# Layer 1's last step with its loads made during the convolution before it, and its additions on two engines

## The chip, the cores and the metric

The kernel runs on one core of a Trainium2 chip, in one launch. The metric is the device time in microseconds (us) of that core. Five engines work side by side, each through its own queue of instructions in order: PE multiplies matrices, DVE (vector), ACT (scalar) and POOL (GpSimd) do elementwise work, SP only issues DMA transfers. ACT and POOL can issue DMAs as well.

## The reference, cut to what matters

The input x has 4 batches of 128 channels and 64 x 64 = 4096 positions. Four layers follow each other.

- Layer 0: a projection, a causal convolution of width 4, a selective scan over the 4096 positions with 16 states for each of 256 inner channels, a gate, an output projection, and the residual. Its result is x1.
- Layer 1: x1 is normalized in groups of channels, an incidence matrix between positions (distance under 16) is built for each batch, and a hypergraph convolution gives `out`. Then comes a batch norm over all batches and positions, and Silu:

```python
mean = jnp.mean(out, axis=(0, 2, 3))
var = jnp.var(out, axis=(0, 2, 3))
y = gamma * (out - mean) * rsqrt(var + eps) + beta
return y * sigmoid(y)          # and x = x1 + this
```

- Layer 2: tokens (positions x channels); linear attention with a layer norm ahead of it, then a mixture of experts.
- Layer 3: windowed attention without softmax, then a mixture of experts.

The mean and variance of layer 1 are over all four batches, so no element of layer 1's result can be made before the convolution of the last batch is done.

## The kernel before

The kernel is written in a framework that records instructions with the tiles they read and write. It takes tiles from pools, places the pools in SBUF (the on-chip memory of 128 partitions), sets the semaphores, and orders each engine's queue when the kernel is built. A tile of a pool takes the room of an earlier one when that one's readers are done. In the built program each DMA also carries one of eight completion counters and is issued only when the DMA before it on that counter has landed, so at most eight are under way.

**Layers 0 and 1** (`layers01`) are interleaved: `layer0` is a generator that makes the scan in steps, `layer1(b)` one that makes the convolution of batch b, and the loop at the end runs layer 0 of batch b + 1 beside layer 1 of batch b. For the last batch (b = 3) layer 0 is done and `layer1(3)` runs alone. Its pools are `aw` (weights and the tiles xn0 to xn7 of the normalized batch), `l0p` (layer 0's tiles, in two to six buffers), `l0bc` (rows of B and C for the scan), `l1t` (layer 1's tiles), and PSUM and DRAM pools. All of them stay open until `layers01` ends.

`layer1(b)` begins with a few small operations for the group norm (`ps_gm`, `ps_gv`, `rstd`), then loads x1 of its batch in eight chunks of 512 columns from DRAM (`xn`, L457, SP's queue) and normalizes each on ACT (L458). A chunk's tile is free when the previous batch has read it last, in `mean` (L631, POOL). The square of chunk 7 (`sq`, L463) is what the first matmul of the convolution waits for, `ps_hb` in `row` (L490). The comparisons, turns, edges and `ps_v` (L622) follow. `finish` stores each chunk of the result to the DRAM tensor hg (L635, SP's queue) and collects statistics.

At the end of `layers01` the batch norm's scale and bias are made from the statistics (`bn`, L666 to L671).

**Layer 1's last step** (`layer1_end`) works in 16 units, one for each batch and 1024 columns. A unit loads o (1024 columns of hg) on ACT's queue (L683) and x (the same columns of x1) on SP's queue (L685), 512 KB each; ACT makes Silu of o with scale and bias (L686); POOL adds o to x (L687); PE turns x in eight transpositions of 128 columns into two PSUM tiles `ps_x` (L692); ACT copies the first PSUM tile and DVE the second into X (L694), the token tile of 64 KB for each partition that layers 2 and 3 work on. Both o and x have three buffers.

Then the first two groups of expert weights of layer 2 are loaded (`load`: `w1` and `w2f`, 1 MB each, on SP's queue, and `b1` on ACT's), and `attn2` starts: its statistics over X (`lnst`, L702), its weight W (L740), normalized tiles z (L779, L781), and projections `ps_qk` (L789).

Of the kernel before, what the change touches and what calls it, by code (L numbers as in the profile page):

```python
# [7 lines left out]
F32 = mybir.dt.float32  # L8
F16 = mybir.dt.float16
FP8 = mybir.dt.float8e4  # L10
AF = mybir.ActivationFunctionType
ALU = mybir.AluOpType
AX = mybir.AxisListType
PSUM = bass.MemoryType.PSUM
DRAM = bass.MemoryType.DRAM

P = 128
B = 4
# [22 lines left out]
class Net:  # L41
# [33 lines left out]
    def layers01(self):  # L75
        nc, tc, a = self.nc, self.tc, self.a
# [9 lines left out]
        LAG = 6 * 2  # L86
        with ExitStack() as ctx:
            wp = ctx.enter_context(tc.tile_pool(name="aw", bufs=1))
            w2 = ctx.enter_context(tc.tile_pool(name="l0p", bufs=2))
            bcp = ctx.enter_context(tc.tile_pool(name="l0bc", bufs=5))  # L90
            tp = ctx.enter_context(tc.tile_pool(name="l1t", bufs=2))
            dp = ctx.enter_context(tc.tile_pool(name="l0d", bufs=3, space=DRAM))
            ip = ctx.enter_context(tc.tile_pool(name="l1i", bufs=1, space=DRAM))
# [2 lines left out]
            ps = ctx.enter_context(tc.tile_pool(name="aps", bufs=4, space=PSUM))  # L96
# [103 lines left out]
            def due(every=False):  # L200
                for w in list(waiting):
                    if every or w[0] <= self.tick:
                        waiting.remove(w)
                        w[1]()
# [445 lines left out]
            for b in range(B):  # L650
                l1 = layer1(b)
                if b < B - 1:
                    done = 0
                    for k in range(states):
                        next(l0, None)
                        self.tick += 1
                        due()
                        while done * states < work * (k + 1):
                            done += next(l1)
                for _ in l1:  # L660
                    self.tick += 1
                    due()
# [7 lines left out]
            nc.vector.tensor_tensor(bn[:, 1:2], bn[:, 2:3], bn[:, 0:1], ALU.mult)  # L670
            nc.vector.tensor_tensor(bn[:, 1:2], gb[:, 1:2], bn[:, 1:2], ALU.subtract)  # L671

    def layer1_end(self):

        nc = self.nc
        with self.tc.tile_pool(name="l1e", bufs=3) as tp, self.tc.tile_pool(
            name="l1eps", bufs=4, space=PSUM
        ) as ps:
            for b in range(B):
                for c in range(4):  # L680
                    sl = slice(c * 1024, (c + 1) * 1024)
                    o = tp.tile([P, 1024], F32, tag="o", name="o")
                    nc.scalar.dma_start(o, self.hg[b][:, sl])  # L683
                    x = tp.tile([P, 1024], F32, tag="x", name="x")
                    nc.sync.dma_start(x, self.x1[b][:, sl])  # L685
                    nc.scalar.activation(o, o, AF.Silu, scale=self.bn[:, 0:1], bias=self.bn[:, 1:2])  # L686
                    nc.gpsimd.tensor_tensor(x, x, o, ALU.add)  # L687
                    for h in range(2):
                        pt = ps.tile([P, 4, P], F32, tag="tr", name="ps_x")
                        for i in range(4):  # L690
                            k = 4 * h + i
                            nc.tensor.transpose(pt[:, i, :], x[:, k * P : (k + 1) * P], self.ident)  # L692
                        k = 8 * c + 4 * h
                        (nc.vector.tensor_copy if h else nc.scalar.copy)(self.X[:, b, k : k + 4, :], pt)  # L694


    def ln_stats(self, sp, b, j0, n, rs=None):
# [543 lines left out]
@with_exitstack  # L1241
def tile_kernel(ctx: ExitStack, tc: tile.TileContext, a, out):
    net = Net(tc, a)
    net.setup(ctx)
    net.layers01()
    xp = ctx.enter_context(tc.tile_pool(name="X", bufs=1))
    net.X = xp.tile([P, B, NB, P], F32, tag="X", name="X")
    net.ew = ctx.enter_context(tc.tile_pool(name="fe", bufs=2))
    net.layer1_end()
    net.ahead = [net.load("L2_ffn", g) for g in range(2)]  # L1250
    net.attn2()
    net.ffn("L2_ffn")
    net.ahead = [net.load("L3_ffn", g) for g in range(2)]
    net.attn3()
    net.ffn("L3_ffn", out)
# [48 lines left out]
```

## Time and profile before

| what | value |
|---|---|
| median of 3 runs | 4328.91 us (4327.95 to 4335.17) |
| profiled execution | 4332.47 us, span of the core 4330.7 us |
| mean granted clock of PE | 0.899 |
| busy, share of the span | PE 83%, DVE 69%, POOL 57%, ACT 48% |
| start of `layer1(3)`: last load of xn issued | 2887.45 us from the span's start |
| last step of layer 1: first Silu to last copy into X | 3337.66 to 3399.92 us |
| first `ps_qk` of layer 2's attention | 3411.09 us |

A line of a group reads: source line, engine, operation, out<-in by the program's names, shapes, count | busy us, mean ns of one | idle time of the engine just before these instructions, and what ended it. A line of the timeline reads: start us, us, engine, line, operation, out<-in, count [idle before <- what ended it]. PEld is PE's weight load, SPq and ACTq the part of SP and ACT that issues DMAs. A line of a stretch reads: from:to, length, busy us of PE, PEld, DVE, ACT and POOL (instructions), granted clock of PE, mean busy share of the 16 DMA engines, GB/s moved.

### The profile page before, as it was taken

How to read it: one execution, taken by the hardware profiler on the slowest of the kernel's cores; microseconds unless marked ns; L12 is line 12 of the kernel's file. 1: busy time of each engine (PE TensorE's matmuls, PEld its weight loads, DVE VectorE, ACT ScalarE, POOL GpSimd, SP SyncE). 2: the span in 40 equal slices, each digit the busy share in tenths (PEclk: the TensorE clock that was granted, in tenths of full speed). 3: DMA queues.
4: the chain of work that ended last, by engine and by line, in shares of the span. 5: the costliest groups of instructions: out<-in, count | busy, mean ns of one | idle time of the engine just before them, and what ended most of it. 6: DMA issues, size and time to landing. Idle time of an engine off the chain costs nothing. (4 is left out here: it accounts for less than half of the span.)

```text
span 4330.7 us, 49179 instructions
## 1 busy us (share of the span) xinstructions
PE 3584.4 (83%) x17367; PEld 2004.0 (46%) x17367; DVE 3001.4 (69%) x4787; ACT 2094.7 (48%) x3551; POOL 2463.2 (57%) x1235
## 2 busy tenths in 40 slices
PE   6877858888896788888778888889998699788788
PEld 2333323444543344453333445445664587447545
DVE  5888889898666998766699987645311665628631
ACT  4555654455544445564454556421231676407621
POOL 5989889887786988778699887730001200003100
PEclk8988978899998799999878999999999799879888
DMA  3444545554364444446444553551214200070045
GB/s 105 148 146 149 150 113 135 134 134 133 102 210 122 122 138 138 141 106 188 138 123 132 144 143 111 163 174 59 79 52 141 94 1 2 29 284 3 2 154 198
DMA packets 261993, 523.96 MB, mean 121 GB/s; under 512 B 22347, under 2 KB 24563, under 8 KB 261747
## 3 DMA queue, kind: packets, MB, share of 16 engines
q1 hardware_dynamic: 250450, 501.45, 39.2%
q10 hardware_dynamic: 11296, 19.37, 1.4%
q8 instruction: 137, 2.24, 0.2%
q14 instruction: 110, 0.89, 0.1%
HBM read 443.15 MB, written 77.59 MB: 120 GB/s over the span
## 5 line engine op out<-in xcount | busy, mean ns | idle before, releaser
L286 POOL TENSOR_TENSOR db<-dx,bt 128x1024 f32<-128x1024 f32 x512 | 1203.0, 2353 | 333.8 <-DVE hs L304 219.2
L304 DVE TENSOR_TENSOR_SCAN hs<-hs,carry,db 128x512 f32<-128x512 f32 x812 | 1035.5, 1283 | 177.0 <-ACT hs L298 94.7
L298 ACT ACTIVATE hs<-dl,A 128x512 f32<-128x512 f32 x1024 | 706.6, 692 | 745.4 <-DVE ho L314 692.2
L499 PE MATMUL ps_g<-xn 128*128 128x512 f32 x1152 | 602.4, 653 | 105.0 <-DVE inc L502 78.3
L321 POOL TENSOR_TENSOR ho_s<-ho_s,ho 128x1024 f32<-128x1024 f32 x288 | 677.1, 2351 | 13.8 <-DVE ho L314 13.2
L314 DVE TENSOR_TENSOR ho<-hs,bt 128x1024 f32<-128x1024 f32 x464 | 563.4, 1214 | 1.6
L522 PE MATMUL ps_ed<-xs,inc 128*128 128x258 f16 x4096 | 512.5, 285 | 18.2 <-ACT inc L515 8.6
L522 PEld LDWEIGHTS <-inc 128*128 128x128 fp8e4 x4096 | 417.3, 102 | 133.9 <-issue 60.5
L502 DVE SCALAR_TENSOR_TENSOR inc<-ps_g,hcl,hb 128x512 fp8e4<-128x512 f32 x576 | 420.4, 736 | 36.7 <-PE ps_g L499 21.0
L499 PEld LDWEIGHTS ps_g<-xn 128*128 128x128 f32 x1152 | 215.3, 204 | 421.2 <-DVE inc L502 189.5
L342 PE MATMUL ps_y<-ho,cst 128*128 128x512 f32 x512 | 272.6, 676 | 111.1 <-POOL ho L310 92.1
L622 PE MATMUL ps_v<-inc_v,es 128*128 128x512 fp8e4 x1536 | 343.1, 383 | 19.2 <-DMA bt<-bcd 17.3
L622 PEld LDWEIGHTS <-es 128*128 128x128 f16 x2048 | 202.6, 99 | 289.1 <-issue 64.0
L515 ACT CAST inc<-ps_t 128x512 fp8e4<-128x512 f32 x448 | 232.1, 600 | 94.3 <-PE ps_t L511 94.2
L224 PE MATMUL ps_c<-xt,wc 128*128 128x512 f32 x512 | 236.5, 616 | 12.4 <-DVE inc L502 6.1
L342 PEld LDWEIGHTS ps_y<-ho,cst 128*128 128x128 f32 x512 | 104.9, 214 | 271.6 <-POOL ho L310 123.0
L528 ACT COPY ed<-ps_ed 128x129 f32<-128x129 f32 x128 | 34.0, 266 | 382.5 <-PE ps_ed L522 382.5
L529 DVE TENSOR_TENSOR ed<-ps_ed,ed 128x129 f32<-128x129 f32 x128 | 36.7, 286 | 211.0 <-ACT ed L528 208.0
L304 DVE TENSOR_TENSOR_SCAN hs<-hs,db 128x512 f32<-128x512 f32 x116 | 141.3, 1223 | 54.3 <-POOL db L286 43.3
L538 POOL TENSOR_TENSOR ed<-ed,rdeg 128x512 f32<-128x512 f32 x32 | 33.2, 1038 | 251.1 <-DVE rdeg L534 251.1
L224 PEld LDWEIGHTS ps_c<-xt,wc 128*128 128x128 f32 x512 | 100.3, 199 | 140.1 <-issue 120.5
L511 PE MATMUL ps_t<-ident,strip 128*128 128x128 fp8e4 x1344 | 114.9, 227 | 51.5 <-DVE ed L529 16.9
(301 smaller groups left out, 5579.2 us busy)
## 6 DMA issues: line engine op xcount, KB each, us to landing
bt<-bcd SPq DMA_DIRECT2D x512, 512.0 KB
inc<-inc SPq DMA_DIRECT2D x192, 256.0 KB
inc_v<-inc SPq DMA_DIRECT2D x96, 512.0 KB
w<-in_L_ffn_weight SPq DMA_DIRECT2D x32, 1024.0 KB
w2f<-in_L_ffn_weight SPq DMA_DIRECT2D x32, 1024.0 KB
strip<-inc SPq DMA_DIRECT2D x84, 256.0 KB
x<-x ACTq DMA_DIRECT2D x32, 256.0 KB
xn<-x SPq DMA_DIRECT2D x32, 256.0 KB
```

The costliest lines, as they stand in the source:

```text
L224: nc.tensor.matmul(s["ps"][h], wc[:, h, j, :], xt[:, j : j + T], start=j == 0, stop=j == 3)
L286: nc.gpsimd.tensor_tensor(db, s["dx"], bc(s["bt", n][:, 0, :], 2), ALU.mult)
L298: act(nc.scalar.activation(hs[:, k, :], s["dl"][:, k, :], AF.Exp, scale=A[:, k, n : n + 1]))
L304: nc.vector.tensor_tensor_scan(to[:, h, :], hs[:, h, :], db[:, h, :], init, ALU.mult, ALU.add)
L314: nc.vector.tensor_tensor(ho, hs, ct, ALU.mult)
L321: nc.gpsimd.tensor_tensor(s["sum", n // G], s["sum", n // G], ho, ALU.add)
L342: nc.tensor.matmul(s["y"][h], self.ident, t[:, h, :], start=False, stop=n == DS - 1 and k == len(terms) - 1,)
L499: nc.tensor.matmul(pq, xn[v // 4][:, v % 4 * P : (v % 4 + 1) * P], xn[c], start=True, stop=True)
L502: nc.vector.scalar_tensor_tensor(inc[:, v, :], pq, hc[:, v : v + 1], hb, ALU.subtract, ALU.is_gt, saturate=False)
L515: later(1, lambda: act(nc.scalar.copy(inc[:, v, :], pt, saturate=False)))
L522: nc.tensor.matmul(pe[:, : 2 * P + 2], inc[:, v, i * P : (i + 1) * P], xs[:, v, :], start=v == 0, stop=v == NB - 1,)
L622: nc.tensor.matmul(pv, es[:, e, k, :], inc[:, e, :], start=e == 0 and k == 0, stop=e == NB - 1 and k == 1,)
```

## The change

The pools `l0p` and `l0bc` move to the other end of SBUF (`side="right"`) and into a stack of their own, which is closed when layer 0 is done, ahead of `layer1(3)`. At that point a new pool `l1e`, in the same place, opens with ten buffers each for o and x, and `reload` issues the loads of the first ten units, all on SP's queue. The other six are issued one by one in `layer1_end`, after each of the first six units. In `layer1_end` the additions of odd units go to DVE, those of even units stay on POOL. The new pool, the PSUM pool of the step and X's pool get `reuse_waits="tile"`: a tile waits for what lay in its own room, not for the whole of the pools before.

```diff
-            w2 = ctx.enter_context(tc.tile_pool(name="l0p", bufs=2))
-            bcp = ctx.enter_context(tc.tile_pool(name="l0bc", bufs=5))
+            only0 = ctx.enter_context(ExitStack())
+            w2 = only0.enter_context(tc.tile_pool(name="l0p", bufs=2, side="right"))
+            bcp = only0.enter_context(tc.tile_pool(name="l0bc", bufs=5, side="right"))
...
+                else:
+
+                    only0.close()
+                    self.reload()
                 for _ in l1:
...
+    def reload(self, first=True):
+        nc = self.nc
+        if first:
+            self.pre = self.tc.tile_pool(name="l1e", bufs=10, side="right", reuse_waits="tile")
+            self.units, self.pool = [], self.pre.__enter__()
+        while len(self.units) < (10 if first else 4 * B):
+            b, c = divmod(len(self.units), 4)
+            sl = slice(c * 1024, (c + 1) * 1024)
+            o = self.pool.tile([P, 1024], F32, tag="o", name="o")
+            nc.sync.dma_start(o, self.hg[b][:, sl])
+            x = self.pool.tile([P, 1024], F32, tag="x", name="x")
+            nc.sync.dma_start(x, self.x1[b][:, sl])
+            self.units.append((o, x))
+            if not first:
+                return
...
     def layer1_end(self):
-        with self.tc.tile_pool(name="l1e", bufs=3) as tp, self.tc.tile_pool(
-            name="l1eps", bufs=4, space=PSUM
-        ) as ps:
-            for b in range(B):
-                for c in range(4):
-                    sl = slice(c * 1024, (c + 1) * 1024)
-                    o = tp.tile([P, 1024], F32, tag="o", name="o")
-                    nc.scalar.dma_start(o, self.hg[b][:, sl])
-                    x = tp.tile([P, 1024], F32, tag="x", name="x")
-                    nc.sync.dma_start(x, self.x1[b][:, sl])
-                    nc.scalar.activation(o, o, AF.Silu, scale=self.bn[:, 0:1], bias=self.bn[:, 1:2])
-                    nc.gpsimd.tensor_tensor(x, x, o, ALU.add)
...
+        with self.tc.tile_pool(name="l1eps", bufs=4, space=PSUM, reuse_waits="tile") as ps:
+            for u in range(4 * B):
+                b, c = divmod(u, 4)
+                o, x = self.units[u]
+                nc.scalar.activation(o, o, AF.Silu, scale=self.bn[:, 0:1], bias=self.bn[:, 1:2])
+                (nc.vector if u % 2 else nc.gpsimd).tensor_tensor(x, x, o, ALU.add)
...
+                self.reload(False)
+        self.pre.__exit__(None, None, None)
...
-    xp = ctx.enter_context(tc.tile_pool(name="X", bufs=1))
+    xp = ctx.enter_context(tc.tile_pool(name="X", bufs=1, reuse_waits="tile"))
```

The transpositions and copies of `layer1_end` are the same as before.

More of the change, by code (lines that the diff above doesn't have):

```diff
@@ L673, in layer1_end @@
     def layer1_end(self):
         nc = self.nc
-        with self.tc.tile_pool(name="l1e", bufs=3) as tp, self.tc.tile_pool(
-            name="l1eps", bufs=4, space=PSUM
-        ) as ps:
-            for b in range(B):
-                for c in range(4):
-                    sl = slice(c * 1024, (c + 1) * 1024)
-                    o = tp.tile([P, 1024], F32, tag="o", name="o")
-                    nc.scalar.dma_start(o, self.hg[b][:, sl])
-                    x = tp.tile([P, 1024], F32, tag="x", name="x")
-                    nc.sync.dma_start(x, self.x1[b][:, sl])
[L686 to L694, printed above, removed]
+        with self.tc.tile_pool(name="l1eps", bufs=4, space=PSUM, reuse_waits="tile") as ps:
[4 more added lines that the diff above has]
+                (nc.vector if u % 2 else nc.gpsimd).tensor_tensor(x, x, o, ALU.add)
+                for h in range(2):
+                    pt = ps.tile([P, 4, P], F32, tag="tr", name="ps_x")
+                    for i in range(4):
+                        k = 4 * h + i
+                        nc.tensor.transpose(pt[:, i, :], x[:, k * P : (k + 1) * P], self.ident)
+                    k = 8 * c + 4 * h
+                    (nc.vector.tensor_copy if h else nc.scalar.copy)(self.X[:, b, k : k + 4, :], pt)
+                self.reload(False)
```

## The prediction

> **What bounds the kernel now.** I read the page first (the slices), then the groups and the timeline of the stretch that the diff rewrites, 3337 to 3400 us, then the stretch where the new loads are placed, 2860 to 2900 us. `layer1_end` runs from its first Silu at 3337.66 us to its last copy into X at 3399.92 us: 62.3 us for 16 units of 1024 columns. The groups of that window (busy, mean ns, idle before and its releaser):
>
> ```profile
> L687 POOL TENSOR_TENSOR x<-x,o 128x1024 f32<-128x1024 f32 x16 | 37.3, 2346 | 25.7 <-ACT o L686 21.4 <-DMA x<-x 4.3
> L692 PE MATMUL ps_x<-cst,x 128*128 128x128 f32 x128 | 31.4, 427 | 35.8 <-POOL x L687 35.8
> L686 ACT ACTIVATE o<-o,bn 128x1024 f32<-128x1024 f32 x16 | 19.6, 1239 | 4.8 <-DMA o<-hg 4.7
> L694 DVE COPY X<-ps_x 128x512 f32<-128x512 f32 x16 | 11.1, 691 | 51.7 <-PE ps_x L692 51.7
> L694 ACT COPY X<-ps_x 128x512 f32<-128x512 f32 x16 | 9.4, 586 | 28.1 <-PE ps_x L692 28.0
> ```
>
> POOL has 37.3 us of additions and waits 25.7 us more, 21.4 of them for Silus and only 4.3 for a load. PE, DVE and ACT wait mostly for POOL or what follows it. The timeline of POOL and ACT shows the beat:
>
> ```profile
> 3358.01 4.66 POOL L687 TENSOR_TENSOR x<-x,o 128x1024 f32<-128x1024 f32 x2 [3.06 <-ACT o L686]
> 3365.73 4.65 POOL L687 TENSOR_TENSOR x<-x,o 128x1024 f32<-128x1024 f32 x2 [3.06 <-ACT o L686]
> ...
> 3364.36 1.24 ACT L686 ACTIVATE o<-o,bn 128x1024 f32<-128x1024 f32 x1
> 3366.09 1.24 ACT L686 ACTIVATE o<-o,bn 128x1024 f32<-128x1024 f32 x1 [0.49 <-DMA o<-hg]
> ```
>
> Two units take 7.72 us: two additions (4.66), then 3.06 in which PE turns the second, ACT copies it and only then, in its queue, makes the next Silu. With three buffers the stage is a ring, not a stream. Both remedies of the change bear on it: a second adding engine shortens the two additions, ten buffers let Silus run ahead.
>
> The start of `layer1(3)`, as stretches (PE, PEld, DVE, ACT, POOL busy; clock; DMA share; GB/s) and timeline:
>
> ```profile
> 2875.00:2880.00 5.00, 5.00 (x25) 2.26 (x24) 0.00 (x0) 0.00 (x0) 0.00 (x0) 1.00 1.04 389
> 2885.00:2890.00 5.00, 0.38 (x2) 0.30 (x2) 3.07 (x8) 1.77 (x4) 1.26 (x1) 0.93 0.88 293
> 2890.00:2895.00 5.00, 0.05 (x1) 0.05 (x1) 0.00 (x0) 4.97 (x9) 0.00 (x0) 0.50 0.02 7
> ...
> 2887.45 0.43 SPq L457 DMA_DIRECT2D xn<-x  x1
> ...
> 2888.49 5.74 ACT L458 ACTIVATE xn<-xn,nmr,rstd 128x512 f32<-128x512 f32 x8 [0.50 <-DVE nmr L452]
> 2894.27 1.15 ACT L463 ACTIVATE sq<-xn 128x512 f32<-128x512 f32 x2
> ```
>
> The last chunk, xn7, is issued at 2887.45 and has landed when ACT takes it at 2893.4; the DMA engines are idle by 2891. PE waits 7.3 us for sq. After that PE is busy 20.00 of 20 us in stretch after stretch, so what delays sq delays everything behind it.
>
> **What the skill says.** (1) GPSIMD Engine Reference, 8. Key points: POOL shares its SBUF interfaces with DVE and contends with DVE instructions that have two SBUF inputs, such as the new additions. The trace does not show it: POOL's L286 takes 2353 ns (median, never over 2383) beside a busy DVE and L687 2346 alone. (2) TensorE: Matmul & The Clock Gate, What's actually happening: PE runs at half clock after some 3.4 us idle until it has been busy as long. The trace agrees on the half (0.50 in most of 3342 to 3400) but took 8 us of work to warm up from 2894.95. (3) ScalarE: Activation LUTs, What ACT_TABLE_LOAD costs: 1283 ns; the trace has 1283.
>
> **The change part by part.** Where instructions go I take from the order of the built program; times are those of the trace of before.
>
> *Up to 2857 us: nothing.* Order and waits of every engine are the same up to SP's first new load; the moved pools change addresses only. 0.
>
> *Loads moved ahead of xn6 and xn7 (cost).* SP's queue now has 20 loads of 512 KB (10.5 MB) after xn5, cut by two stores of hg and followed by xn6 and xn7. Before, 3 MB of such loads (half on ACT's queue) and 4 MB of FFN weights stood there. The stores wait for POOL's L631, which ends at 2872.3 and 2887.04. By the first, 6 loads are done. The next 9 (4.7 MB at the 390 GB/s seen in 2875 to 2880: 12.1 us, from about 2874) end at 2886. Behind the second store come 5 loads, 2.62 MB, and 0.5 MB of xn: 3.15 MB, 8.1 us, from 2889.4 (2 us after issue; estimated from xn7 before, which with 2 MB ahead of it was in by 2891). So xn7 lands near 2897.5, ACT finishes it at 2898.6 instead of 2894.2: **+4.4 us** on the path. Bounds: +2 if the rate is the 426 GB/s seen in places, +10 if it is 250.
>
> *FFN weights (4 MB) leave this place* for the end of `layer1_end`; the first (1 MB) waits for the last store of hg and moves from 3338 to 3341, ahead of the six late units. Those are issued as units 0 to 5 free their buffers, 3341 to 3353, and at 1.35 us each have landed by about 3357; ACT wants the first of them at about 3360: 0. The other 3 MB stand before attention's W on SP's queue: 7.9 us, W near 3366, wanted by DVE after 3380: 0. Were these 15 us late, W would hold the projections.
>
> *The stage itself (gain).* POOL keeps 8 additions (18.8 us). DVE gets 8; not shown before, the nearest row is L314, also two SBUF inputs of 1024: 1214 ns, 9.7 us. Bounds: 1.1 to 2.4 (as slow as POOL); up to 2.4 it still fits, so it adds under 3. A pair of units now costs ACT 2 x (1.239 + 0.586) = 3.65, PE 16 transposes, 2 x 1.97 = 3.94 at half clock, DVE 1.21 + 2 x 0.69 and four statistics of the next stage (0.28 each), 3.7, POOL 2.35. PE at half clock is the dearest: 8 x 3.94 = 31.5. Ahead of it the way to the first transposition, 3341.38 - 3337.66 = 3.7; behind it the last copy, and the sqrt with table load (1.6) that the order puts ahead of ACT's last copy: 1.1 of both are not hidden; and 2 for the new wait: an addition on DVE waits for ACT's Silu with DVE's copies queued behind it, and stands itself behind a copy that waits for PE; PE, with four PSUM buffers, waits for those copies. 38.3 us against 62.3: **-24.0**. Bounds: 34.5 if PE warms up (ACT: 29.2 + 1.6 + waits), 42 if DVE's queue holds more.
>
> *Entry to attention.* Before, 11.2 us from the last copy to the first qk matmul (3411.09): 16 statistics, then W, then z. Now the first batch's statistics lie inside the stage, but in DVE's order W's preparation stands after eight z and the second batch's statistics, and PE's z transposes behind W's: about 1.9 + 4.6 + 3.5 + 2.5 = 12.5: **+1.3**. In exchange ACT, which is saturated up to 3462, has two table loads fewer (225 to 223 in the program, 2.6) and some 1.4 of z behind it: **-4.0**, bounds 0 and -6.
>
> Sum: +4.4 - 24.0 + 1.3 - 4.0 = **-22.3 us**. The profiled execution took 4332.47 (span 4330.7), so 4310.2; it lies 3.6 above the median of the runs, so in medians 4328.91 - 22.3 = 4306.6, **4307**.
>
> **The rivals.**
> - *PE warms up in the stage:* its gaps shrink below 1 us, ACT is the bound, 34.5 us. For it: PE has work waiting. Against: the one time that it warmed up in this stage, at 3387.7, it had fallen back by 3391. -26.1: 4303.
> - *DVE's order makes a ring again:* each addition of DVE stands behind the copy of the unit before, which waits for PE: 2 x 1.97 + 0.69 + 1.21 = 5.84 a pair, 46.7 + 3.7 = 50.4 us. For it: the order puts copies ahead of additions; against: ten Silus can run ahead. -10.2: 4319.
> - *The prefetch gives nothing by itself*, since only 9 us of waits ended with a DMA. This only says that the gain is the ring's; it changes no number.
> - *Slower:* SP's queue. xn6 and xn7 wait behind the loads, and all of `layer1(3)` behind them. The delay is the time of the last 3.15 MB less 3.7 us; it decides when it passes the 26.7 us gained, that is below 104 GB/s (the page's mean is 120, but at low demand). At 80 GB/s: 39.4 us, +35.7, so +9: 4338. Against it: 390 GB/s in the same stretch with the same kind of loads.
>
> **How the numbers follow.** Main case 0.62 (4307), warm PE 0.16 (4303), DVE's ring 0.14 (4319), slower 0.04, anything else 0.04. Range 4297 to 4321: the best ends (34.5 us, +2, -6) give -30 or so, the bad ones (42 us, +10, attention 0) -8. 0.2% is 8.7 us, about what a measurement of this kernel can tell from no change; below 4320.2 are the main case, the warm one and most of the ring: faster 0.88, same 0.08, slower 0.04.
>
> **What would show it.** Right: xn7's ACT at 2898 to 2899; stage near 38 us with POOL's idle gone as main wait and PE or ACT nearly full; the six late loads never ending a wait; the first qk near 3393 against 3411. Wrong: sq later than 2905; DVE additions well over 1.3 us or POOL's over 2.4; DVE waiting for PE with ACT idle; W ending a wait at the entry to attention.

## The result, and the profile after

The median is 4313.53 us (4305.70 to 4315.92) against 4335.17 for the kernel before (4327.95 to 4339.50), measured side by side: ratio 0.9949, 95% interval 0.9933 to 0.9966. A second measurement gave 4313.00 against 4331.63, 0.9955 (0.9937 to 0.9973). The forecast of -22.3 us met -21.6 in the medians; the 4307 itself is 6.5 low because the kernel before came out 6.3 higher than in its first three runs. The interval of the ratio is -15 to -29 us, so that the two agree to 0.7 us is in part luck.

The profiled execution after took 4305.70 us (span 4303.6) against 4332.47 (4330.7) before. It is the fastest of its five, so the two spans differ by more, 27.1 us, than the medians. By stretch (`ps_l`, L1110, is the first matmul of the mixture of experts that follows the attention):

| stretch, us | before | after | difference | predicted |
|---|---|---|---|---|
| start to `rstd` of `layer1(3)` | 2887.7 | 2887.4 | -0.4 | 0 |
| `rstd` to first `sq` | 6.5 | 12.4 | +5.9 | +4.4 |
| `sq` to first Silu (convolution) | 443.4 | 441.4 | -2.0 | 0 |
| first Silu to last copy into X | 62.3 | 36.9 | -25.4 | -24.0 |
| last copy to first `ps_qk` | 11.2 | 9.1 | -2.1 | +1.3 |
| first `ps_qk` to first `ps_l` (attention) | 260.3 | 259.9 | -0.4 | -4.0 |
| from there to the end | 659.3 | 656.6 | -2.7 | 0 |

First the stage. These are the groups of the kernel after from 3337 to 3380 us (L704 is the addition that was L687, L709 the transposition, L711 the copies):

```profile
L709 PE MATMUL ps_x<-cst,x 128*128 128x128 f32 x128 | 22.7, 348 | 19.1 <-POOL x L704 15.3 <-DVE x L704 3.7
L704 POOL TENSOR_TENSOR x<-x,o 128x1024 f32<-128x1024 f32 x8 | 21.7, 2713 | 11.7 <-ACT o L703 11.7
...
L703 ACT ACTIVATE o<-o,bn 128x1024 f32<-128x1024 f32 x16 | 19.2, 1238 | 0.0
L704 DVE TENSOR_TENSOR x<-x,o 128x1024 f32<-128x1024 f32 x8 | 12.5, 1558 | 3.2 <-ACT o L703 3.2
L711 ACT COPY X<-ps_x 128x512 f32<-128x512 f32 x16 | 9.3, 580 | 7.6 <-PE ps_x L709 7.6
```

None of these waits ends with a DMA any more. ACT's Silus show no wait of their own, but they stand in ACT's queue with its copies, which wait 7.6 us for PE; PE waits 19.1 us, mostly for POOL's additions, and POOL still waits 11.7 us for Silus. So part of the ring is left. The transpositions shrank from 427 to 348 ns each: PE warmed up. But the additions grew: POOL's mean went from 2346 to 2713 ns, and DVE's is 1558 where 1214 was the price. The timeline of POOL and DVE shows how:

```profile
3342.47 5.66 POOL L704 TENSOR_TENSOR x<-x,o 128x1024 f32<-128x1024 f32 x2 [2.27 <-ACT o L703]
3365.07 2.91 POOL L704 TENSOR_TENSOR x<-x,o 128x1024 f32<-128x1024 f32 x1 [0.38 <-ACT o L703]
```

```profile
3343.55 2.34 DVE L704 TENSOR_TENSOR x<-x,o 128x1024 f32<-128x1024 f32 x1 [2.94 <-ACT o L703]
3358.88 0.67 DVE L721 BATCH_NORM_STATS2 lnst<-X 128x6 f32<-128x128 f32 x3
...
3366.47 1.54 DVE L727 TENSOR_TENSOR lnnm<-lnst 128x16 f32<-128x16 f32 x1
...
3379.70 0.18 DVE L727 TENSOR_TENSOR lnnm<-lnst 128x16 f32<-128x16 f32 x1
```

POOL's first addition, from 3342.47, would end at 3344.82 with its usual 2.35. DVE's begins at 3343.55 and takes 2.34: until 3344.82 it stands, then comes its own 1.1. POOL's second begins then, stands for that time, and ends at 3348.13: two in 5.66 instead of 4.70. Plainer still is a DVE operation of 16 columns with two inputs in SBUF, `lnnm`, which takes 0.18 us when POOL has no addition under way (at 3379.70): at 3366.47 it takes 1.54, and ends at 3368.01 where POOL's addition ends (3365.07 + 2.91 = 3367.98). They take turns, instruction by instruction; statistics, with one input, are not held up beside POOL (three in 0.67 us at 3358.88).

The stretches of the stage from 3350 us on (PE, PEld, DVE, ACT, POOL busy; clock; DMA share; GB/s):

```profile
3350.00:3360.00 10.00, 6.71 (x43) 5.86 (x42) 8.33 (x18) 8.39 (x11) 6.72 (x3) 0.83 0.97 352
3360.00:3370.00 10.00, 5.23 (x40) 4.11 (x38) 9.83 (x20) 8.06 (x10) 5.27 (x2) 1.00 1.03 397
3370.00:3378.00 8.00, 5.60 (x24) 4.71 (x24) 6.33 (x16) 4.81 (x7) 3.06 (x1) 0.57 0.45 150
3378.00:3388.00 10.00, 2.66 (x8) 1.81 (x9) 10.00 (x57) 4.96 (x12) 0.00 (x0) 0.62 0.00 0
```

PE reaches full clock within 3350 to 3360 and falls back at the end; DVE, with the statistics of attention between its copies, fills up (9.83 of 10, and 10.00 after the last copy).

Then the price, at the start of `layer1(3)`: ACT's and SP's timelines.

```profile
2888.12 4.33 ACT L459 ACTIVATE xn<-xn,nmr,rstd 128x512 f32<-128x512 f32 x6 [0.50 <-DVE nmr L453]
2898.23 1.52 ACT L459 ACTIVATE xn<-xn,nmr,rstd 128x512 f32<-128x512 f32 x2 [5.77 <-DMA xn<-x]
2899.78 1.15 ACT L464 ACTIVATE sq<-xn 128x512 f32<-128x512 f32 x2
```

```profile
2886.70 0.32 SPq L636 DMA_DIRECT2D hg<-rb  x1
...
2889.71 0.98 SPq L458 DMA_DIRECT2D xn<-x  x2
```

xn6 and xn7 are issued at 2889.71, behind five of the new loads; ACT has six chunks done and waits 5.77 us for the last two. In the stretch between, ACT was busy for 4.97 of 5 us before and the DMA idle (0.02); now ACT is busy for half of it and the DMA for all:

```profile
2890.00:2895.00 5.00, 0.00 (x0) 0.00 (x0) 0.00 (x0) 2.46 (x4) 0.00 (x0) 0.50 1.00 344
```

### The profile page after: what moved, and what is told of

Same layout as the page of the kernel before. It is cut to its first block, busy times and chain, and to the rows that moved or that the text cites. A ratio compares the mean times of both kernels' runs of the same rounds, so it can differ in the third digit from the quotient of the medians.

```text
span 4303.6 us, 49161 instructions
## 1 busy us (share of the span) xinstructions
PE 3572.2 (83%) x17367; PEld 1996.2 (46%) x17367; DVE 3013.9 (70%) x4795; ACT 2092.4 (49%) x3549; POOL 2446.7 (57%) x1227
## 5 line engine op out<-in xcount | busy, mean ns | idle before, releaser
L315 DVE TENSOR_TENSOR ho<-hs,bt 128x1024 f32<-128x1024 f32 x464 | 563.3, 1214 | 1.6
L503 DVE SCALAR_TENSOR_TENSOR inc<-ps_g,hcl,hb 128x512 fp8e4<-128x512 f32 x576 | 420.4, 736 | 37.2 <-PE ps_g L500 21.6
```

Of the source, the lines that this page charges most:

```text
L315: nc.vector.tensor_tensor(ho, hs, ct, ALU.mult)
L503: nc.vector.scalar_tensor_tensor(inc[:, v, :], pq, hc[:, v : v + 1], hb, ALU.subtract, ALU.is_gt, saturate=False)
```

## The experiments

Stages and fronts below are taken from each kernel's profile; "the stage" is always first Silu to last copy into X. The whole time varies by 10 us and more to either side from run to run for any kernel here (in the profiles the clock of PE in the last part, 3650 to 4290 us, ran from 0.81 to 0.89), so effects of a few us are read from the stretches, not from the ratios.

### All additions on POOL

```diff
-                (nc.vector if u % 2 else nc.gpsimd).tensor_tensor(x, x, o, ALU.add)
+                nc.gpsimd.tensor_tensor(x, x, o, ALU.add)
```

> The changed kernel with all 16 additions on POOL, early loads and ten buffers kept. Theory (the gain is that the ring of three buffers is broken, and the rest is the bound of one engine): POOL runs its additions almost without a gap, 16 x 2.35 = 37.6 us, plus 3.7 ahead and 2.7 behind: the last step of layer 1 takes about 44 us (62.3 before, 36.9 after), additions on POOL take 2346 ns each since no addition runs on DVE, and the whole is 5 to 8 us over the changed kernel. Rival (the second adding engine brings the gain): the step stays at 55 to 62 us and POOL goes on waiting over 20 us for Silus.

Stage 48.9 us (3341.4 to 3390.3); ratio to before 0.9989 (0.9976 to 1.0003), no gain clear of the noise. It lies between the theories: the early loads, with POOL as in the kernel before, take 13.4 of 62.3 us, and 5.7 of that is given back at the front. The whole is some 17 us over the changed kernel by the ratios, where 5 to 8 was expected; the stage accounts for 12. POOL's group:

```profile
L704 POOL TENSOR_TENSOR x<-x,o 128x1024 f32<-128x1024 f32 x16 | 37.4, 2365 | 8.1 <-ACT o L703 8.1
```

Alone, POOL's addition is 2.34 to 2.42 us again: the 2713 came from DVE's.

### Two engines, without the early loads

```diff
-                    nc.gpsimd.tensor_tensor(x, x, o, ALU.add)
+                    (nc.vector if c % 2 else nc.gpsimd).tensor_tensor(x, x, o, ALU.add)
```

(in the kernel before)

> The kernel before with only one edit: additions of odd units on DVE; three buffers, loads and pools as before. Theory (ring): a buffer is bound for a load (some 3.5 us), Silu 1.24, addition 1.2 or 2.35 and transpositions 2, about 9 us for three units, so the last step takes 45 to 52 us, its start is as before (sq at 2894), and the whole is 8 to 15 us under before. Rival (the second engine brings the gain): the step takes 37 to 40 us as in the changed kernel. Other rival: nothing gained, 60 us, since the waits are those of ACT's queue.

Stage 59.3 us, ratio 0.9998 (0.9981 to 1.0016). My theory was wrong: a second engine alone gives 3 us.

```profile
L687 POOL TENSOR_TENSOR x<-x,o 128x1024 f32<-128x1024 f32 x8 | 19.7, 2472 | 37.9 <-ACT o L686 23.8 <-DMA x<-x 8.5 <-PE ps_x L692 5.6
L686 ACT ACTIVATE o<-o,bn 128x1024 f32<-128x1024 f32 x16 | 19.4, 1238 | 8.7 <-DMA o<-hg 8.7
```

POOL has half the additions and waits for ACT all the same. So the time of the additions alone did not set the beat of the stage before.

### The loads behind `layer1(3)`'s own

```diff
                     only0.close()
-                    self.reload()
                 for _ in l1:
                     self.tick += 1
                     due()
+            self.reload()
```

> The changed kernel with reload() called after layer1(3) is recorded instead of ahead of it, so that xn6 and xn7 stand on SP's queue right behind the two stores of hg, ahead of five to fourteen of the early loads. Theory (position on SP's queue costs the start of layer1(3)): ACT normalizes xn0 to xn7 without a wait, sq starts 5 to 6 us earlier than in the changed kernel (2894 instead of 2900), nothing else changes, and the whole is about 5 us under the changed kernel. Rival (the 10.5 MB themselves slow the transfer of xn, wherever they stand): sq stays later than 2897.

```profile
2892.45 5.74 ACT L459 ACTIVATE xn<-xn,nmr,rstd 128x512 f32<-128x512 f32 x8 [0.50 <-DVE nmr L453]
2898.22 1.15 ACT L464 ACTIVATE sq<-xn 128x512 f32<-128x512 f32 x2
```

The eight chunks are normalized in one run and `rstd` to `sq` is 6.5 us, as before; the stage is 37.2. Ratio 0.9943 (0.9924 to 0.9963). The 5.9 us at the front are the order of SP's queue, shown.

### All additions on DVE

```diff
-                (nc.vector if u % 2 else nc.gpsimd).tensor_tensor(x, x, o, ALU.add)
+                nc.vector.tensor_tensor(x, x, o, ALU.add)
```

> The changed kernel with all 16 additions on DVE. Theory A (additions on DVE and POOL at the same time slow each other, as both read both inputs from SBUF): every addition takes 1.21 us on DVE, with no long ones. Theory B (DVE is nearly full in the step): DVE has 16 x 1.21 + 16 x 0.69 = 30.4 us plus statistics, so statistics are put off, the step takes 34 to 40 us, and the first qk matmul comes at about the time of the changed kernel or up to 6 us later. Rival to A: mean above 1.4 us as in the changed kernel (1.56), then POOL is not the cause.

```profile
L704 DVE TENSOR_TENSOR x<-x,o 128x1024 f32<-128x1024 f32 x16 | 19.3, 1218 | 1.8 <-ACT o L703 1.8
```

```profile
3351.00:3361.00 10.00, 6.00 (x47) 4.74 (x46) 10.00 (x13) 9.85 (x13) 0.00 (x0) 1.00 1.01 393
```

Stage 30.8 us, shorter than with two engines and than the 34 to 40 of theory B, and all 16 additions flat (1.21 to 1.23), as theory A has it. Ratio 0.9929 (0.9905 to 0.9953). ACT (9.85 of 10), DVE (10.00) and the DMA (393 GB/s) are now full at once.

### POOL busy with data of its own

Sixteen additions of two private tiles on POOL, beside the kernel with both corrections (loads late, all additions on DVE):

```diff
+            s = op.tile([P, 1024], F32, tag="s", name="own_s")
+            t = op.tile([P, 1024], F32, tag="t", name="own_t")
...
                 nc.vector.tensor_tensor(x, x, o, ALU.add)
+                nc.gpsimd.tensor_tensor(s, s, t, ALU.add)
```

> The kernel with both corrections, and beside it POOL adds two SBUF tiles of its own (128x1024, s = s + t, 16 times, nothing waits for them), so that POOL works through the stage on data that no other engine touches. The result is unchanged. Theory (DVE and POOL slow each other when both add two SBUF operands, whatever the data): DVE's additions, flat at 1.22 us without it, become 1.2 to 2.35 with a mean of 1.8 or more, POOL's go from 2.35 to as much as 3.35; the stage grows from 30 to 36 to 42 us, since DVE has then 16 x 0.6 = 10 us more work; copies from PSUM and statistics (one SBUF operand) stay at 0.69 and 0.28. Rival (the long additions of the changed kernel were long because POOL and DVE handed units and buffers to each other, or because of the DMA loads): additions flat at 1.22, stage at 30.

```profile
L711 POOL TENSOR_TENSOR own_s<-own_s,own_t 128x1024 f32<-128x1024 f32 x16 | 50.6, 3162 | 1.3
L710 DVE TENSOR_TENSOR x<-x,o 128x1024 f32<-128x1024 f32 x16 | 44.9, 2816 | 1.8 <-ACT o L709 1.8
```

```profile
3362.00 2.77 DVE L710 TENSOR_TENSOR x<-x,o 128x1024 f32<-128x1024 f32 x1
3364.69 0.68 DVE L718 COPY X<-ps_x 128x512 f32<-128x512 f32 x1
3365.29 2.77 DVE L710 TENSOR_TENSOR x<-x,o 128x1024 f32<-128x1024 f32 x1
```

The theory holds and was too mild: DVE's addition goes from 1.22 to 2.82, the stage from 29.8 to 56.4, the ratio to before to 0.9981 (0.9969 to 0.9993); no tile is shared, so it is neither hand-over nor buffers. One addition of each engine takes 3.29 us (3362.00 to 3365.29), where one after the other takes 1.22 + 2.35 = 3.57: together they do 8% more than in turns. The copies, from PSUM, stay at 0.68. Both engines read as nearly full in this stage (10.00 and 9.77 of 10 from 3365 to 3375): busy time contains the standing.

### Both corrections together, twice

```diff
-                    self.reload()
...
+            self.reload()
...
-                (nc.vector if u % 2 else nc.gpsimd).tensor_tensor(x, x, o, ALU.add)
+                nc.vector.tensor_tensor(x, x, o, ALU.add)
```

> Both corrections together: the loads behind all of layer1(3)'s own loads, and all 16 additions on DVE. Theory (the two effects are independent, since they lie in different stretches): rstd to sq 6.5 us as in before, the stage (first Silu to last copy) 31 us, DVE additions flat at 1.21, the first ps_qk about 6 us ahead of the kernel with DVE alone; against the changed kernel -6 at the front and -6 in the stage, about -12 us, 0.997 of it. Rival: what is saved in the stage is given back in attention, since ACT and DVE are full there: then the time from the last copy to the first ps_l is longer by up to 6 us and the whole is only -6.

> The kernel with both corrections again, as the control of the run beside it and to see whether its first time, 25 us below the changed kernel where its two stretches account for 13, holds. Expected: 12 to 14 us below the changed kernel, ratio to before 0.992; rstd to sq 6.5 us, stage 30 us. Rival: 0.9905 again, then something outside the two stretches is shorter as well.

This is below both kernels: medians 4287.30 and 4293.60, ratios to before 0.9905 (0.9886 to 0.9925) and 0.9928 (0.9900 to 0.9956). The first interval is clear of the changed kernel's (0.9937 to 0.9973), the second overlaps it. `rstd` to `sq` 6.5 us, stage 29.8 both times; last copy to `ps_qk` 8.8, attention 259.8 both times: nothing is given back, so the first rival falls. The two stretches are worth 7.7 + 6.9 = 14.6 us against the changed kernel's own profile, measured beside the first of the two; the ratios say 12 to 22. In both profiles `rstd` itself comes early (2876.2 and 2878.2; 2881.6 to 2894.3 in those of the other kernels). The place of SP's new loads does not explain it: three other kernels have them in the same place, and `rstd` at 2886.7 (five buffers), 2891.7 (loads late, two engines) and 2894.3 (POOL on data of its own). So it varies from run to run.

The changed kernel, measured beside the first of these:

> The changed kernel itself, for the comparison on the same chip. Expected: the same ratio to before as in its first measurement, 0.995; rstd to sq about 12 us, the stage about 37 us; POOL's additions spread over 2.3 to 3.4 us and DVE's over 1.2 to 2.3, each long where the other runs.

Ratio 0.9955, `rstd` to `sq` (the front) 14.2 us, stage 36.7, additions 2.35 to 3.35 on POOL and 1.21 to 2.34 on DVE: as in its first measurement, the front 1.8 longer.

### Five buffers

The kernel with both corrections, with five buffers instead of ten:

```diff
-            self.pre = self.tc.tile_pool(name="l1e", bufs=10, side="right", reuse_waits="tile")
+            self.pre = self.tc.tile_pool(name="l1e", bufs=5, side="right", reuse_waits="tile")
...
-        while len(self.units) < (10 if first else 4 * B):
+        while len(self.units) < (5 if first else 4 * B):
```

> As the kernel with both corrections, but with five buffers for o and x instead of ten: five units loaded ahead, eleven issued as buffers come free. Theory (the ring needs little depth once the additions are on DVE; a unit's o and x are used some 4 us after its Silu, a load of both takes 2.7 us at 390 GB/s and 2 us of latency): units 5 on are issued at the pace of the stage, 1.9 us a unit, but their loads take 2.7 us a unit, so the DMA becomes the bound for the eleven late units: 11 x 2.7 = 30 us from the first free buffer, the stage 33 to 36 us, with some waits for DMA. Rival: five buffers are a ring again, the stage is 45 us or more. Third: the loads keep up and the stage stays at 31.

Stage 51.6 us, ratio 0.9959 (0.9938 to 0.9980). The size is the second theory's, the reason is none of the three: only 1.6 us of waits end with a DMA.

```profile
L709 PE MATMUL ps_x<-cst,x 128*128 128x128 f32 x128 | 25.9, 377 | 30.3 <-DVE x L704 26.8 <-DVE lnnm L727 3.4
...
L703 ACT ACTIVATE o<-o,bn 128x1024 f32<-128x1024 f32 x16 | 19.4, 1238 | 1.6 <-DMA o<-hg 1.6
...
L721 DVE BATCH_NORM_STATS2 lnst<-X 128x6 f32<-128x128 f32 x71 | 16.0, 279 | 0.0
...
L703 ACT ACT_TABLE_LOAD x4 | 5.1, 1283 | 0.1
L733 ACT ACT_TABLE_LOAD x4 | 5.1, 1283 | 0.1
```

The order of the queues is written when the kernel is built. With five buffers it puts 71 statistics of attention into the stage, 64 of them ahead of DVE's last addition (4 with ten buffers, all behind it), and four square roots between ACT's Silus and copies, with a table load each and one back to Silu after the first three. PE then waits 26.8 us for DVE's additions. So the depth seems to act through the order that it leads to; this is read from the profile, and no run kept five buffers with the order of ten.

### The pools' waits

The changed kernel without `reuse_waits="tile"` in its three places:

```diff
-name="l1e", bufs=10, side="right", reuse_waits="tile")
+name="l1e", bufs=10, side="right")
...
-name="l1eps", bufs=4, space=PSUM, reuse_waits="tile")
+name="l1eps", bufs=4, space=PSUM)
...
-tc.tile_pool(name="X", bufs=1, reuse_waits="tile")
+tc.tile_pool(name="X", bufs=1)
```

> The changed kernel without reuse_waits in the three places, so the new loads, the PSUM tiles and X wait for all of the pools that lay in their room. Theory: nothing (within 2 us): the order of every engine is the same, only the first load of o and the first copy into X carry more waits, for things that are long done; first copy into X at the same 4 us after the first Silu. Rival: the first load of o waits for the end of layer 0's last readers and moves the 20 loads, xn6 and xn7 by some us, or the first copy into X waits for the last stores of hg (landed about 3341), so the stage starts up to 3 us later.

Ratio 0.9951 (0.9932 to 0.9971), front 12.9 us, stage 36.7: no effect, as expected.

### DVE alone, and depth, without the early loads

In the kernel before, all additions on DVE:

```diff
-                    nc.gpsimd.tensor_tensor(x, x, o, ALU.add)
+                    nc.vector.tensor_tensor(x, x, o, ALU.add)
```

> The kernel before with one edit: all 16 additions on DVE, the loads where they were, three buffers. It tells what the engine alone is worth without the early loads. Theory (the two engines' gain of 3 us in the earlier run was small because of contention and of the ring; with flat additions of 1.22 the ring's pair is 2 x 1.22 + 3.06 = 5.5 plus a copy of DVE that stands between, 6.2): 8 x 6.2 = 50 us for the stage instead of 62, -12 us in all. Rival: the loads bound it, since 13 units of 1 MB come at 2.7 us each while o waits for ACT to issue and land (3 us seen): 13 x 3.5 = 46 or more, with most of ACT's waits ended by DMA. Other rival: nothing gained, 58 to 62, the ring's other steps are the bound.

Stage 59.8 us, ratio 0.9986 (0.9975 to 0.9996): the other rival, almost nothing. DVE's timeline, with PE's beside it, gives the beat:

```profile
3362.55 0.69 DVE L694 COPY X<-ps_x 128x512 f32<-128x512 f32 x1 [2.12 <-PE ps_x L692]
3363.16 1.22 DVE L687 TENSOR_TENSOR x<-x,o 128x1024 f32<-128x1024 f32 x1
3366.44 0.69 DVE L694 COPY X<-ps_x 128x512 f32<-128x512 f32 x1 [2.06 <-PE ps_x L692]
```

```profile
3364.43 1.97 PE L692 MATMUL ps_x<-cst,x 128*128 128x128 f32 x8 [1.92 <-DVE x L687]
```

Each addition stands behind the copy of the unit before, which waits for PE, which waits for the addition: 1.22 + 1.97 + 0.69 = 3.9 us a unit, with PE at half clock (0.53 on average over the stage). It is the ring that the prediction named as a rival, here once for every unit.

The same with ten buffers, still opened when the convolution is done:

```diff
-        with self.tc.tile_pool(name="l1e", bufs=3) as tp, self.tc.tile_pool(
+        with self.tc.tile_pool(name="l1e", bufs=10) as tp, self.tc.tile_pool(
```

> As the run beside it, with ten buffers for o and x but still opened after the convolution is done: depth without the early loads. Theory (the loads then start after the last store of the convolution, at about 3338, and 16 MB come at 390 GB/s): 16 x 2.7 = 43 us from the first load, the first Silu about 4 us later than now, last copy at 3340 + 43 + 4, so 47 to 50 us from where the first Silu stood before; ACT's waits end with DMA. If so, what the early loads buy is 16 to 19 us over depth alone. Rival: the transfers are done in parallel with others faster than that and the stage is 35.

```profile
3344.33 0.33 ACTq L683 DMA_DIRECT2D o<-hg  x1
...
3351.53 1.24 ACT L686 ACTIVATE o<-o,bn 128x1024 f32<-128x1024 f32 x1 [2.76 <-DMA o<-hg]
...
3374.65 0.59 ACT L694 COPY X<-ps_x 128x512 f32<-128x512 f32 x1 [3.36 <-PE ps_x L692]
3374.71 0.33 ACTq L683 DMA_DIRECT2D o<-hg  x1
```

Stage 62.0 us, first Silu 5.9 us later after `rstd` than before, ratio 1.0017 (1.0005 to 1.0028): slightly slower. This run changes more than the depth: with three buffers the first three units' loads were issued at about 2866 us, during the convolution; with ten none is issued ahead of 3332.8. My 47 to 50 missed because ACT issues the loads of o from its own queue, in order with its Silus and copies, and is never more than three units ahead, so ten buffers never fill. From 3338 to 3360 the DMA is full (380 to 408 GB/s, with x among it, which SP issues far ahead), and the Silu at 3351.53 waits for an o issued at 3344.33; from 3370 on the DMA moves 112 GB/s or less, and each load of o stands behind a copy that waits for PE. What depth would do with the loads on SP's queue was not tried.

## Why the prediction was right, and where it was not

The stage in all six combinations:

| additions on | three buffers, o on ACT's queue | ten buffers, loads early, all on SP's queue |
|---|---|---|
| POOL | 62.3 | 48.9 |
| POOL and DVE | 59.3 | 36.9 |
| DVE | 59.8 | 30.8 |

The right column differs from the left in three things at once: depth, the time of the loads (on the left only those of the first three units are made during the convolution) and the queue of o. No run took the three apart; ten buffers with o on ACT's queue, no early load and the additions on DVE gave nothing (62.0).

- **What bounds the kernel.** The reading of the ring was right, its link was not. I took POOL's 21.4 us of waits for ACT, against 4.3 for a load, as a sign that a faster addition would pay. Two engines or a faster one without the loads take 2.4 to 3.0 us off; the loads (with their depth and queue) with POOL unchanged 13.4; both together 25.4 or 31.5. The wait for a Silu was in part a wait for the Silu's own load or its place in ACT's queue, one step further back. So the third rival, that the prefetch gives nothing by itself, was wrong for the stage.
- **The stage, -24.0.** Measured -25.4, two errors against each other. "PE at half clock is the dearest, 31.5": PE warmed up in the middle of the stage and was busy for 22.7, as the first rival said. Its place was taken by the additions: "POOL keeps 8 additions (18.8)" was 21.7, and DVE's "9.7" was 12.5, in sum 5.7 us more. All additions on DVE end that and take 6.1 us off the stage. So that the sum came out within 1.4 us is luck. Two of the signs that the prediction named for being wrong came true: DVE's additions took 1.56 us on average (over 1.3) and POOL's 2.71 (over 2.4). And of those for being right, two did not: POOL's main wait is still for Silus, and neither PE (22.7 of 36.9 us) nor ACT (28.7) is nearly full.
- **The failed step is the price of DVE's addition.** I took L314 as "also two SBUF inputs"; its `hs` lies in PSUM (pool `l0a`). So that row, and POOL's L286 beside it, say nothing of two SBUF inputs, and "The trace does not show it" set aside a sentence of the Trainium skill that was right. The skill's page Trainium Architecture — The Big Picture, What this means for kernel authors, calls what the two engines share "an exclusive lock (not a bandwidth split)"; the 1.54 us of `lnnm` agree, and the 3.29 us for a pair in the run with private data nearly so (3.57 in full turns). Its page Perfetto Trace Analysis, Optimizing Scalar/DVE Operations, adds that offloading between the two "might not help": two engines against DVE alone, 36.9 against 30.8 us.
- **The loads ahead of xn6 and xn7, +4.4.** Right in kind, and shown by moving them. It measured +5.9, and from 5.7 to 7.7 in the five profiles with this order of the queue: ACT took xn6 and xn7 at 2898.23 instead of the 2897.5 at which xn7 was to land. The term that was small is the rate: the DMA moved 344 GB/s from 2890 to 2895, where I used 390; 3.15 MB take 9.2 us instead of 8.1.
- **Entry, +1.3.** Measured -2.1. I added four pieces of DVE's and PE's work as if each began where the last ended (12.5). DVE worked through them without a gap (10.00 of 10), but W's preparation began 4.9 us after the last copy, not 6.5, and from there to `ps_qk` it took 4.2, not 6.0, since z and W overlapped.
- **Attention, -4.0.** Measured -0.4. There were three table loads fewer than before in it (12 for 15), but ACT is busy for 200.0 of 269 us from the last copy to the first `ps_l`, and PE for 246.4 (246.9 before): what ACT saves lies beside PE. "Saturated up to 3462" did not carry over to the whole stretch. The misses of entry and attention cancel: -2.5 against -2.7.
- **The weights and the six late loads, 0.** Right: none of the stage's waits shown above ends with a DMA.
- **Slower by SP's queue.** At 344 GB/s from 2890 to 2895 the rate was far above the 104 at which it would have decided.

## What to carry to other kernels

Before work is split between POOL and DVE, look at where each operand lies: where both have two SBUF inputs, as here, the two take turns, and the faster engine alone did better. Where the waits run in a ring, a wait's releaser is only its last link, and changing one link (the engine, the buffers) did little here until the loads were early, deep and off ACT's queue as well. Loads made early should be put behind the loads that the work under way still needs, and after a change of depth the order of the queues should be read again, since it may be that, and not the depth itself, that moves the time.

## What was not expected of the hardware

- A DVE addition of 16 columns took 1.54 us instead of 0.18 when POOL was in the middle of an addition, and ended with it: the turn is a whole instruction. Large additions of both engines gave 3.29 us a pair against 3.57 one after the other.
- Both engines count as busy while they stand (10.00 and 9.77 of 10 us with POOL on data of its own). A high share of POOL and DVE is no proof of work.
